# A gating stage over sorted edges: BF16 one-hot products in place of a dense count matrix

## The chip, the cores and the metric

The kernel runs on one core of one Trainium2 chip. The metric is the device time in microseconds (us) of one execution. The engines' short names are those of the profile: PE is TensorE (PEld its weight loads), DVE is VectorE, ACT is ScalarE, POOL is GpSimd, SP is SyncE, which here only issues DMAs (SPq is its queue, POOLq that of GpSimd). SBUF is the on-chip memory of 128 partitions, PSUM the accumulator that PE writes, HBM the memory outside.

## The reference

The program is two layers of a graph network over N = 3125 nodes with D = 256 features. Each layer adds to x a graph convolution and an attention mixer, and then a mixture of experts. Only the first layer's expert part, `_L0_ffn_ref`, is computed in another way by the change; cut to what matters:

```python
x = x + _L0_gnn_ref(xn, edge_index, ...) + _L0_mix_ref(xn[None], ...)[0]
x = x + _L0_ffn_ref(_layernorm(x)[None], ...)[0]

def _L0_ffn_ref(x, ..., edge_index):          # M = 3125 nodes, 65536 edges, 4 heads, 4 experts
    h = (x_flat @ W_gat).reshape(M, HEADS, NUM_EXPERTS)
    src = concatenate([edge_index[0], arange(M)]); dst = concatenate([edge_index[1], arange(M)])
    a_src = (h * att_src).sum(-1);  a_dst = (h * att_dst).sum(-1)
    e = leaky_relu(a_src[src] + a_dst[dst], negative_slope=0.2)
    ee = exp(e - segment_max(e, dst)[dst])
    alpha = ee / (segment_sum(ee, dst)[dst] + 1e-16)
    agg = segment_sum(h[src] * alpha[:, :, None], dst).reshape(M, 16) + b_gat
    scores = layernorm(agg).reshape(M, HEADS, NUM_EXPERTS).mean(1)
    topk_s, topk_i = top_k(scores, 2);  w = softmax(topk_s)
    for ei in range(NUM_EXPERTS):
        g = where(topk_i == ei, w, 0.0).sum(-1)
        hh = gelu(x @ W1[ei] + b1[ei])                       # 256 -> 512
        out = out + g[..., None] * (hh @ W2[ei] + b2[ei])    # 512 -> 256
```

So every node attends to the sources of its incoming edges and to itself; the result only decides which two of four experts a node takes and with what weights. The edge indices of this part run to 4095: a source above 3124 counts as node 3124, and an edge with a destination above 3124 is dropped. The mixer (`_L0_mix_ref`) is four transformer blocks with linear attention: Q, K, V from a layer norm, and a feed-forward part of 1024 hidden units.

## The kernel before

Nodes stand in tiles of 128: NT = 25 tiles `t`, the last with 53 rows, and NG = 7 groups `g` of four tiles (512 columns). All stages run one after the other on the core, and the engines overlap inside a stage. Instructions are issued in order on each engine; a planner places them.

**Start and mixer** (0 to 1732 us). x is loaded and normed for all groups; then four layers `l`, each a QKV part (25 tiles, `beside()` after each tile) and a feed-forward part (`experts_hidden`, then the second product with `add_row`; `beside(2)` after each tile). One call `beside(n)` is n slots, 75 slots a layer, 300 in all. Two generators are advanced there beside the mixer's own work, at a rate per slot that `OF_GRAPH` and `OF_GATING` set:

- `graph.places` and `graph.blocks` count the 100000 edges of the graph convolution into a matrix A (BF16, HBM) with one-hot products: per block of eight columns DVE makes `g_ol` and `g_oh` (L544), PE multiplies (L551), ACT copies out (L555), a DMA stores.
- `windows(eb, tail)` does the 65536 gating edges, 512 columns of 128. For each column DVE compares a key with five columns of keys, `junk<-kr,keyb,w_before` (L324), which tells how often an edge occurs; `counted` turns this into a place; POOL adds the value into the N x N count matrix C2 in HBM by an indirect DMA (L336). The DMAs go in windows of five, each after the one before has landed. `clear_own` zeroes C2 first (L619, 25 DMAs).

**Graph convolution** (1732 to 2020 us). xn is read back from HBM (`xg<-xn_d`, L214) and split into three BF16 parts `xb` (L980 to L985); a branch `if_more()` covers counts that BF16 can't hold; then `sums` multiplies them by A (L920).

**Gating and experts of layer 0** (2020 to 3112 us), in three steps:

1. Each group is normed and turned, its features go to HBM (`xf_d`), and `hg` = x W_gat, a_src and a_dst are made.
2. "gat0", 2109 to 2484 us: for each of the 25 target tiles the rows of C2 are read (`cnt`, L1167), ACT makes a penalty (`pen`, L1171), and DVE takes for four heads the maximum of a_src over the sources (L1174). Beside this `experts()` computes all four experts for all nodes (L235 with `xfg`, L1100) and stores the results in HBM (`y_d`).
3. "gat1", 2484 to 3112 us: for all pairs of target and source columns and all heads the softmax terms are made densely: ACT (L1260, L1277), POOL (L1261) and DVE (L1266, L1284) on 128 x 1024 tiles, counts turned by PE (L1282), sums by PE (L1296). `weighed` makes the gates and adds the experts' results, read back from `y_d`, with diagonal products (L1468, L1469).

**Layer 1** (3112 us to the end) is a second graph convolution, mixer and expert part.

The rate of the two side generators is all there is to it in the loop:

```python
for i, (it, w) in enumerate(((counting, OF_GRAPH), (gating, OF_GATING))):
    if not (clearing and i):
        share[i] += w * n
    while share[i] >= 1.0:
        share[i] -= 1.0
        next(it, None)
```

Of the kernel before, what the change touches and what calls it, by code (L numbers as in the profile page):

```python
# [8 lines left out]
F32 = mybir.dt.float32  # L9
# [8 lines left out]
P = 128  # L18
# [21 lines left out]
WIDE = 5  # L40
BLOCK = 6 * WIDE
COLS = 32
MANY = 9
# [12 lines left out]
GT = 3  # L56
OF_GRAPH = 1.05
OF_GATING = 0.45
# [33 lines left out]
def tile_gps(ctx: ExitStack, tc: tile.TileContext, a, out):  # L92
# [31 lines left out]
    masks = {}  # L124
    for w in (32, 64):
        m = ctile([P, P], f"mask{w}")
        V.memset(m, 0.0)
        for i in range(P // w):
            V.memset(m[i * w:(i + 1) * w, i * w:(i + 1) * w], 1.0)
        masks[w] = m  # L130
# [3 lines left out]
    xf_d = dram.tile([P, 2, N], F32, name="xf_d")  # L134
# [4 lines left out]
    pq_d = dram.tile([10, N], F32, name="pq_d")  # L139
    y_d = dram.tile([NT, P, 4, D], F32, name="y_d")  # L140
# [87 lines left out]

    def experts_hidden(ps, pool, w1, xT, n, nhb, bias, bufs=10):
# [69 lines left out]
    class Edges:  # L299

        after = mybir.DependencyInfo(mybir.DependencyClass.Sync, mybir.DependencyReason.DATA)

        def __init__(self, ep, w_before, dump, key, width, used, rows, mat, tag):
            self.ep, self.w_before, self.dump = ep, w_before, dump
            self.key, self.used, self.rows = key, used, rows
            self.flat = mat.rearrange("(n o) -> n o", o=1)
            self.val = ep.tile([P, width], F32, name=f"val{tag}", tag=f"val{tag}")
            self.idx = key[:, :].bitcast(I32)
            self.before, self.started = [], []
            self.width, self.made = width, 0  # L310

        def prepare(self, cols):

            ep, key = self.ep, self.key
            c0, c1 = self.made, min(self.made + cols, self.width)
            for c in range(c0, c1, WIDE):
                k = min(WIDE, c1 - c)
                kr = ep.tile([P, WIDE * P], F32, name="kr", tag="kr", bufs=2)
                nc.sync.dma_start(kr[:, :k * P], self.rows[c * P:(c + k) * P]
                                  .rearrange("(o f) -> o f", o=1).to_broadcast([P, k * P]))  # L320
                for j in range(k):
                    junk = ep.tile([P, WIDE * P], BF16, name="junk", tag="junk", bufs=1)
                    u = (WIDE - 1 - j) * P
                    V.scalar_tensor_tensor(junk[:, :k * P], kr[:, :k * P], key[:, c + j:c + j + 1],  # L324
                                           self.w_before[:, u:u + k * P], op0=OP.is_equal, op1=OP.mult,
                                           accum_out=self.val[:, c + j:c + j + 1])
                if c + k < c1:
                    yield
            counted(key, self.val, self.dump, c0, c1 - c0)
            self.made = c1  # L330
            yield

        def scatter(self, c, end):

            assert c < self.made
            s = G.indirect_dma_start(  # L336
                out=self.flat, out_offset=bass.IndirectOffsetOnAxis(ap=self.idx[:, c:c + 1], axis=0),
                in_=self.val[:, c:c + 1], in_offset=None, compute_op=OP.add)

            first, last = c == 0, c == self.used - 1  # L340
            if not first and not last:
                for o in self.started:
                    tc.declare_no_dep(s.ins, o.ins, reason="no index twice in a window")
# [4 lines left out]
            if end:  # L348
                self.before, self.started = self.started, []
# [1697 lines left out]
```

## Time and profile before

| what | value |
|---|---|
| time, median of 3 runs | 4495.22 us (4488.73 to 4502.27) |
| the profiled execution | 4501.24 us, of which the span from first to last instruction is 4499.5 us |
| granted PE clock, mean | 0.923 |
| busy share of the span | PE 85%, DVE 57%, ACT 35%, POOL 35% |
| first QKV product starts at | 67.3 us |
| mixer's QKV parts, layers 0 to 3 | 67 to 216, 534 to 629, 952 to 1055, 1379 to 1468 us |
| gating's compares (L324) run from, to | 249.9 to 1278.7 us |
| gating's indirect DMAs (L336) run from, to | 256.9 to 1624.8 us |

Times are counted from the first instruction of the profiled execution. A row of a stage gives, for each engine, the us in which it was busy in that stretch and in brackets how many instructions. A row of a group gives line, engine, operation, what is written and read, shapes and count; then busy us in all, mean ns of one; then the idle time just before such instructions and what ended it. A busy PE isn't a PE at its peak: one of its matmuls overlaps the next, so the distance from start to start is shorter than the length shown.

### The profile page before, as it was taken

The numbers are of one execution on the slowest core, as the hardware profiler recorded it, in microseconds if no ns is written. First come the engines' busy times: TensorE is split into PE (matmuls) and PEld (weight loads), VectorE is DVE, ScalarE is ACT, GpSimd is POOL, SyncE is SP. The second block draws the span as 40 slices with busy tenths as digits, with TensorE's granted clock in tenths as the row PEclk, the third lists the DMA queues.
The fourth block names the chain that finished last, engine by engine and source line by source line (L and its number), as shares of the span: only waits on it lengthen the run. The fifth ranks groups of instructions, "written<-read, shape, count | busy, mean of one in ns | idle before, by whom it ended". The sixth has DMA issues, their size and how long they took to land. (4 is left out here: it accounts for less than half of the span.)

```text
span 4499.5 us, 48886 instructions
## 1 busy us (share of the span) xinstructions
PE 3841.9 (85%) x17539; PEld 2271.2 (50%) x17630; DVE 2580.8 (57%) x6382; ACT 1566.8 (35%) x2431; POOL 1563.1 (35%) x1044
## 2 busy tenths in 40 slices
PE   3589979997999898988996465767899989999998
PEld 2366655665666564445664222323554444444577
DVE  7687887878766322024999899998710313223331
ACT  3232432343234322013544698984300210000133
POOL 0345555656555620000000588884000310000134
PEclk9799989998999999997998687988999999999999
DMA  9946555564545213225554322324622122211366
GB/s 275 269 58 54 61 43 52 59 56 47 53 30 46 4 3 102 70 71 195 182 195 127 127 91 87 110 89 153 200 72 75 54 77 60 59 54 56 109 166 161
DMA packets 432666, 433.19 MB, mean 96 GB/s; under 512 B 203827, under 2 KB 367958, under 8 KB 427304
## 3 DMA queue, kind: packets, MB, share of 16 engines
q1 hardware_dynamic: 345826, 413.75, 35.9%
q0 software_dynamic: 86576, 16.09, 7.4%
q8 instruction: 146, 2.39, 0.2%
q14 instruction: 118, 0.97, 0.1%
HBM read 300.31 MB, written 136.76 MB: 97 GB/s over the span
## 5 line engine op out<-in xcount | busy, mean ns | idle before, releaser
L336 POOL DMA_INDIRECT C<-valb,keyb x512 | 812.5, 1587 | 632.8 <-DMA C<-valb,keyb 298.5
L1261 POOL TENSOR_TENSOR ex<-ex,pqb 128x1024 f32<-128x1024 f32 (+1 forms) x150 | 353.6, 2378 | 943.4 <-ACT ex L1260 943.1
L324 DVE SCALAR_TENSOR_TENSOR junk<-kr,keyb,w_before 128x640 bf16<-128x640 f32 x512 | 446.8, 873 | 9.5 <-DMA kr<-keys_b 7.0
L920 PE MATMUL ag<-chb,Hb 128*128 128x512 bf16 (+1 forms) x1752 | 412.9, 386 | 17.2 <-DMA chb<-A 15.2
L920 PE MATMUL ag<-chb,xb 128*128 128x512 bf16 (+3 forms) x1907 | 397.9, 365 | 15.6 <-DMA chb<-A 12.9
L1174 DVE CUSTOM_DVE_ANT_0 am<-asb,pen 128x1664 f32<-128x1664 f32 (+3 forms) x200 | 357.2, 1786 | 51.7 <-ACT pen L1171 41.8
L872 PE MATMUL o<-w,hid 128*128 128x256 f32 (+1 forms) x1600 | 380.1, 386 | 0.0
L235 PE MATMUL mm<-hT,w 128*128 128x512 f32 (+1 forms) x896 | 375.1, 566 | 1.8 <-ACT hid L238 1.8
L1296 PE MATMUL pa<-ex,hgp 128*32 128x512 f32 (+1 forms) x1200 | 196.1, 731 | 179.1 <-DVE ex L1284 178.8
L238 ACT ACTIVATE hid<-mm,fm 128x512 f32<-128x512 f32 (+1 forms) x336 | 210.5, 631 | 395.6 <-PE mm L235 393.1
L1284 DVE SCALAR_TENSOR_TENSOR ex<-ex,ct 128x2048 f32<-128x2048 f32 (+1 forms) x150 | 336.2, 2277 | 6.8 <-PE ct L1282 5.0
L872 PEld LDWEIGHTS o<-w,hid 128*128 128x128 f32 (+1 forms) x1600 | 295.5, 191 | 52.5 <-issue 10.5
L1277 ACT ACTIVATE ex<-ex,as 128x1024 f32<-128x1024 f32 x300 | 319.8, 1134 | 2.7 <-DVE ex L1266 2.6
L920 PEld LDWEIGHTS <-xb 128*128 128x128 bf16 (+1 forms) x2100 | 183.4, 97 | 231.5 <-issue 22.3
L920 PEld LDWEIGHTS <-Hb 128*128 128x128 bf16 (+1 forms) x2100 | 184.1, 99 | 226.9 <-issue 33.7
L235 PEld LDWEIGHTS mm<-hT,w 128*128 128x128 f32 x896 | 159.5, 195 | 163.2 <-issue 149.9
L1576 POOL DMA_INDIRECT slots<-rb,r_ati x50 | 50.4, 1007 | 510.5 <-DVE rb L1569 402.9
L769 PE MATMUL mm<-wqkv,hT 128*128 128x512 f32 (+1 forms) x400 | 209.8, 642 | 7.4 <-DVE kmax L783 6.4
L551 PE MATMUL gc<-g_oh,g_ol 128*128 128x50 bf16 (+1 forms) x1589 | 177.4, 273 | 36.3 <-ACT g_st L555 35.0
L235 PE MATMUL mm<-xfg,f0w 128*128 128x512 f32 (+1 forms) x448 | 189.5, 568 | 16.2 <-DMA xfg<-xf_d 11.4
L555 ACT ACTIVATE g_st<-gc 128x400 bf16<-128x400 f32 x192 | 95.1, 503 | 292.9 <-DMA A<-g_st 144.0
L551 PEld LDWEIGHTS <-g_ol 128*128 128x128 bf16 (+1 forms) x1589 | 157.8, 146 | 68.9 <-issue 55.8
(489 smaller groups left out, 6189.2 us busy)
## 6 DMA issues: line engine op xcount, KB each, us to landing
C<-zero SPq DMA_DIRECT2D x25, 1528.0 KB
cnt<-C SPq DMA_DIRECT2D x24, 1562.5 KB
cd<-C SPq DMA_DIRECT2D x36, 1024.0 KB
kr<-keys_b SPq DMA_DIRECT2D x102, 320.0 KB
f1w<-in_f_w_dram SPq DMA_DIRECT2D x56, 512.0 KB
slots<-blank SPq DMA_DIRECT2D x15, 1820.0 KB
chb<-A SPq DMA_DIRECT2D x48, 397.2 KB
A<-g_st SPq DMA_DIRECT2D x24, 768.0 KB
```

Source lines behind the costliest of these rows:

```text
L235: T.matmul(ph[:, :n], lhsT=w1[:, k, hb * P:(hb + 1) * P], rhs=xT[:, k, :n], start=(k == 0), stop=(k == 1))
L238: S.activation(h[:, :n], ph[:, :n], AF.Gelu, bias=bias[hb])
L324: V.scalar_tensor_tensor(junk[:, :k * P], kr[:, :k * P], key[:, c + j:c + j + 1], self.w_before[:, u:u + k * P], op0=OP.is_equal, op1=OP.mult,
L336: s = G.indirect_dma_start(out=self.flat, out_offset=bass.IndirectOffsetOnAxis(ap=self.idx[:, c:c + 1], axis=0), in_=self.val[:, c:c + 1], ...
L551: T.matmul(p[:, j, :], lhsT=lo[:r, :, j], rhs=hi[:r, :h, j], start=True, stop=True)
L769: T.matmul(pqk[:r], lhsT=h, rhs=wqkv[:, k, 0:512], start=(k == 0), stop=(k == 1))
L872: T.matmul(po[:r], lhsT=hid[hb][:, j * P:j * P + r], rhs=w2[:, hb, :], start=(hb == 0), stop=False)
L920: T.matmul(acc[fb, g][:, :n], lhsT=Xb[:r, s, i, fb * P:(fb + 1) * P], rhs=ch[:r, at:at + n], start=first, stop=last, skip_group_check=g == ...
L1174: V.tensor_tensor_reduce(out=junk[:r, :w], in0=asb[:r, h, c0:c1], in1=pen[:r, :w], scale=1.0, scalar=-3.0e38, op0=OP.subtract, op1=OP.max, ...
L1261: G.tensor_tensor(e, e, pq[:r, h, :n], op=OP.add)
L1277: S.activation(ex[:r, h, :n], ex[:r, h, :n], AF.Exp, bias=sc)
L1284: V.scalar_tensor_tensor(e4, e4, 1.0, ct[:r, None, :m].to_broadcast([r, 4, m]), op0=OP.min, op1=OP.mult)
```

## The change

In words, along the program:

- **C2 and its clearing leave the common path.** `Edges`, `windows`, `clear_own` and the ordered adding DMAs go. Instead `Buckets` sorts the gating edges by pair of tiles: the key of an edge is (tile of dst) x 29 + (tile of src), times 128, and each key owns 128 places (640 where the source tile is the last) of a table `btab` in HBM. `split` makes keys and in-tile offsets (a word dst x 128 + src). `places` runs over 128 steps of WIDE = 4 columns, in three parts each: DVE compares keys (as before, now four columns wide, all that came earlier counting 1) and makes one-hot rows `od`, `os_` of the tile numbers; PE turns `od` (four products), ACT copies the result, PE multiplies `od` with `os_` (four) and the turned rows with the running counts (four); DVE adds the two ranks and updates the counts. Every 32 columns the places are computed and POOL writes the words with 32 indirect DMAs, which add nothing and have no order among them (512 in all, as before). The last 32 come after the last step.
- **The rates.** `OF_GATING` goes from 0.45 to 1.4; gating has 25 parts for every 32 columns, 400 in all. Up to slot `HEAD` = 18 only the graph's generator runs, at 2.5 a slot.
- **The start.** The load of x is issued first; only group 0 is normed before the loop, the others inside `normal`; the loading and first steps of the lists move into the generator `begun`.
- **Before the first graph convolution** the table is read back (`wf<-btab`), taken apart into two BF16 rows of in-tile offsets, stored (`low_d`), and one of them turned (`to_low`). In the order of SP's queue the load of `wf` stands after two of the seven loads of `xg` and waits for the last indirect DMA.
- **Step 1 of the gating** keeps the features in SBUF (`xT`) and computes expert 0 for each group beside it.
- **gat0 and gat1 go.** `sparse()` runs over 725 chunks of 128 places, six at a time (121 blocks): `fetched` loads two rows of offsets to all partitions and makes one-hot matrices (`hot`, twice, and `put`, 128 x 768 BF16); `gathered` picks a_src, h and a_dst with two BF16 products per chunk (the tables are split into three BF16 parts), and DVE, ACT (Exp) and POOL make the terms, with the node's own edge's e in the place of the maximum; `added` sums a chunk into its target tile with a third product. The blocks are stepped from `keep_beside` beside the last group of expert 0 and expert 1; the order of the built program has 45 of 121 blocks between these experts' products, and 76 after them.
- **Experts.** Results of experts 0 and 1 stay in SBUF (`y`); the gates are made for all tiles at once; experts 2 and 3 run last, and `weigh` adds them straight from PSUM with the gate as a scale. The bias is a small BF16 product in each tile (`ones3`, `rows0`).
- **A branch** `if_more(dense)` holds the dense attention (`in_full`) for inputs in which a bucket overflows or a_src lies beyond 30.
- ACT's activation tables: the built program of the changed kernel has 50 table loads, before 12; of the 50, 43 stand at Gelu (25) and at the new Exp (18).

The core of the diff:

```diff
-WIDE = 5
-BLOCK = 6 * WIDE
+WIDE = 4
...
-OF_GATING = 0.45
+OF_GATING = 1.4
+CHUNKS = 29
...
+SOME = 6
+HEAD = 18
...
+        def places(self, ps, w_before):
...
+            for c0 in range(0, E1 // P, COLS):
...
+                    kr = ep.tile([P, WIDE * P], F32, name="kr", tag="kr", bufs=2)
+                    nc.sync.dma_start(kr, keys_g[c * P:(c + WIDE) * P]
+                                      .rearrange("(o f) -> o f", o=1).to_broadcast([P, WIDE * P]))
+                    for j in range(WIDE):
+                        junk = ep.tile([P, 5 * P], BF16, name="junk", tag="junk", bufs=1)
+                        u = (WIDE - 1 - j) * P
+                        V.scalar_tensor_tensor(junk[:, :WIDE * P], kr, self.key[:, c + j:c + j + 1], w_before[:, u:u + WIDE * P],
+                                               op0=OP.is_equal, op1=OP.mult, accum_out=rank[:, c - c0 + j:c - c0 + j + 1])
+                    od, os_ = (ep.tile([P, WIDE, HIS], BF16, name=f"b_{nm}", tag=f"b_{nm}", bufs=2) for nm in ("od", "os"))
+                    for o, of in ((od, self.dh), (os_, self.sh)):
+                        V.tensor_tensor(o, self.of[:, None, :].to_broadcast([P, WIDE, HIS]),
+                                        of[:, c:c + WIDE, None].to_broadcast([P, WIDE, HIS]), op=OP.is_equal)
+                    yield
+                    for j in range(WIDE):
+                        T.transpose(turned[:, j * P:(j + 1) * P], od[:, j, :], ident_b)
+                    to = ep.tile([P, WIDE * P], BF16, name="b_to", tag="b_to", bufs=1)
+                    S.activation(to[:HIS], turned[:, :WIDE * P], AF.Copy)
+                    for j in range(WIDE):
+                        T.matmul(made, lhsT=od[:, j, :], rhs=os_[:, j, :], start=(j == 0), stop=(j == WIDE - 1))
+                    yield
+                    for j in range(WIDE):
+                        T.matmul(found[:, j, :], lhsT=to[:HIS, j * P:(j + 1) * P],
+                                 rhs=self.counts[:HIS].rearrange("p k h -> p (k h)"), start=True, stop=True)
+                    was = ep.tile([P, 5 * P], BF16, name="b_was", tag="junk", bufs=1).bitcast(F32)
+                    was = was[:, :2 * HIS * WIDE].rearrange("p (w k h) -> p w k h", w=WIDE, k=2)
+                    V.tensor_tensor(was, found.rearrange("p w (k h) -> p w k h", k=2),
+                                    os_[:, :, None, :].to_broadcast([P, WIDE, 2, HIS]), op=OP.mult)
+                    more4 = ep.tile([P, WIDE], F32, name="b_more", tag="b_more")
+                    V.tensor_reduce(more4, was.rearrange("p w k h -> p w (k h)"), axis=AX.X, op=OP.add)
+                    r4 = rank[:, c - c0:c - c0 + WIDE]
+                    V.tensor_tensor(r4, r4, more4, op=OP.add)
+                    n, parts2 = self.total[:HIS], self.counts[:HIS]
+                    V.tensor_tensor(n, n, made, op=OP.add)
+                    V.tensor_copy(parts2[:, 0, :], n)
+                    V.tensor_tensor(parts2[:, 1, :], n, parts2[:, 0, :], op=OP.subtract)
+                    yield
...
+                for c in range(c0, c0 + COLS):
+                    d = G.indirect_dma_start(
+                        out=btab.rearrange("(n o) -> n o", o=1),
+                        out_offset=bass.IndirectOffsetOnAxis(ap=self.key[:, c:c + 1].bitcast(I32), axis=0),
+                        in_=self.word[:, c:c + 1], in_offset=None)
...
+            nc.sync.dma_start(wf[:, :full, :], btab[0:full * P * P].rearrange("(b p s) -> p b s", p=P, s=P))
...
+                nc.sync.dma_start(low_d[i].rearrange("(b p s) -> p b s", p=P, s=P), wb[:, i])
...
+            def fetched(k0, n):
...
+                    nc.sync.dma_start(row[:, :n * P], low_d[i:i + 1, k0 * P:(k0 + n) * P].to_broadcast([P, n * P]))
...
+                    V.tensor_scalar(h[:, :n * P], row[:, :n * P], own[:, 0:1], None, op0=OP.is_equal)
...
+                V.tensor_tensor(put[:, :, :n], all6[:, :, :n], to_low[:, None, k0:k0 + n].to_broadcast([P, P, n]),
+                                op=OP.is_equal)
...
+            def gathered(k0, n, hot, put):
...
+                for j in range(n):
+                    dh, k = (k0 + j) // CHUNKS, (k0 + j) % CHUNKS
+                    T.matmul(pg[:, 60 * j:60 * j + 60], lhsT=hot[1][:, j * P:(j + 1) * P],
+                             rhs=tables[0][:, min(k, HIS - 1)], start=True, stop=True)
+                    T.matmul(pg[:, 360 + 24 * j:384 + 24 * j], lhsT=hot[0][:, j * P:(j + 1) * P],
+                             rhs=tables[1][:, dh], start=True, stop=True)
...
+                V.tensor_reduce(vs[:, :n], pg[:, :60 * n].rearrange("p (j k v) -> p j v k", k=3, v=20), axis=AX.X, op=OP.add)
+                V.tensor_reduce(vd[:, :n], pg[:, 360:360 + 24 * n].rearrange("p (j k v) -> p j v k", k=3, v=8),
                                 axis=AX.X, op=OP.add)
+                e = vs[:, :n, 0:4]
+                V.tensor_tensor(e, e, vd[:, :n, 0:4], op=OP.add)
+                V.scalar_tensor_tensor(e, e, 0.2, e, op0=OP.mult, op1=OP.max)
+                V.tensor_tensor(e, e, vd[:, :n, 4:8], op=OP.subtract)
+                S.activation(e, e, AF.Exp)
+                m = vs[:, :n, 4:20].rearrange("p j (h v) -> p j h v", h=4)
+                V.tensor_tensor(m, m, e[:, :, :, None].to_broadcast([P, n, 4, 4]), op=OP.mult)
...
+                S.activation(mp3[:, :n, 0], vs[:, :n], AF.Copy)
+                G.tensor_tensor(rest[:, :n], vs[:, :n], mp3[:, :n, 0], op=OP.subtract)
+                S.activation(mp3[:, :n, 1], rest[:, :n], AF.Copy)
+                G.tensor_tensor(mp3[:, :n, 2], rest[:, :n], mp3[:, :n, 1], op=OP.subtract)
...
+                    T.matmul(acc[dh], lhsT=put[:, :, j], rhs=mp3[:, j].rearrange("p k v -> p (k v)"),
+                             start=(k == 0), stop=(k == CHUNKS - 1))
...
+            def keep_beside(e):
+                def done(t, r, po):
+                    nonlocal share1
+                    S.activation(y[:r, e, t, :], po[:r], AF.Copy)
+                    share1 += each1
+                    while share1 >= 1.0:
+                        share1 -= 1.0
+                        next(beside1, None)
+                return done
...
+            def weigh(e):
+                def done(t, r, po):
+                    V.scalar_tensor_tensor(xs[:r, t, :], po[:r], gt[:r, t, e:e + 1], xs[:r, t, :], op0=OP.mult, op1=OP.add)
```

## The prediction

> **What bounds the kernel now.** I read the busy time by stages first, since no engine bounds the whole span: two stretches of the mixer's feed-forward part, then the two gating steps.
>
> ```profile
> core 0: us, PE busy (x) PEld busy (x) DVE busy (x) ACT busy (x) POOL busy (x), PEclk, DMA share, GB/s
> 1510.00:1730.00 220.00, 218.40 (x841) 138.57 (x840) 48.04 (x171) 56.71 (x98) 72.81 (x47) 1.00 0.16 5
> 1055.00:1379.00 324.00, 289.51 (x1343) 198.10 (x1341) 230.86 (x711) 96.82 (x168) 194.18 (x123) 0.93 0.49 45
> 2109.00:2484.00 375.00, 326.37 (x1173) 211.35 (x1171) 362.61 (x455) 175.42 (x253) 0.00 (x0) 0.95 0.50 170
> 2484.00:3112.00 628.00, 404.97 (x2338) 165.62 (x2338) 560.38 (x524) 521.54 (x518) 467.40 (x261) 0.82 0.32 100
> ```
>
> The mixer is bound by PE: its last feed-forward part, with neither graph nor gating beside it, is 99% PE; with both it takes 324 us, PE 89%. gat0 is bound by DVE (363 of 375), with the four experts' products beside it at no cost; gat1 by DVE with ACT and POOL close behind. Next I read the costliest groups, for what goes and for durations of what comes:
>
> ```profile
> L324 DVE SCALAR_TENSOR_TENSOR junk<-kr,keyb,w_before 128x640 bf16<-128x640 f32 x512 | 446.8, 873 | 9.5 <-DMA kr<-keys_b 7.0
> L1174 DVE CUSTOM_DVE_ANT_0 am<-asb,pen 128x1664 f32<-128x1664 f32 (+3 forms) x200 | 357.2, 1786 | 51.7 <-ACT pen L1171 41.8
> L1284 DVE SCALAR_TENSOR_TENSOR ex<-ex,ct 128x2048 f32<-128x2048 f32 (+1 forms) x150 | 336.2, 2277 | 6.8 <-PE ct L1282 5.0 <-ACT ex L1277 1.4
> L235 PE MATMUL mm<-xfg,f0w 128*128 128x512 f32 (+1 forms) x448 | 189.5, 568 | 16.2 <-DMA xfg<-xf_d 11.4 <-ACT hid L238 4.6
> L1100 PE MATMUL o<-f0w,hid 128*128 128x256 f32 (+1 forms) x800 | 181.7, 380 | 1.5 <-ACT hid L238 0.8 <-ACT yo L1102 0.7
> L551 PE MATMUL gc<-g_oh,g_ol 128*128 128x50 bf16 (+1 forms) x1589 | 177.4, 273 | 36.3 <-ACT g_st L555 35.0 <-ACT hT L203 0.9
> L544 DVE TENSOR_TENSOR g_ol<-g_all,g_lo 128x1024 bf16<-128x1024 bf16 (+1 forms) x199 | 136.0, 683 | 0.0
> L927 PE MATMUL ag<-ident_b,xb 128*128 128x128 bf16 x144 | 8.9, 219 | 0.0
> L434 POOL DMA_INDIRECT g_t<-tab,g_idx x25 | 24.3, 972 | 19.4 <-DVE g_skip L473 9.3 <-issue 6.4 <-DVE g_t L506 3.1
> L238 ACT ACT_TABLE_LOAD x6 | 7.7, 1283 | 0.1
> ```
>
> A small BF16 product costs 8.9/144 = 0.06 us (L927) to 177.4/1589 = 0.11 (L551, weights read with a stride). An expert costs PE (189.5 + 181.7)/4 = 93 us.
>
> **A, the start: -70.** The first QKV product comes at 67.3 us; DVE waits there for a late row (17.57 us in the timeline):
>
> ```profile
> 60.01 0.43 DVE L681 CAST row_part<-row_x 128x512 bf16<-128x512 f32 x1 [17.57 <-DMA row_x<-in_mix_rows_dram]
> ...
> 60.47 0.35 DVE L682 TENSOR_SCALAR rows<-row_part,row_pick 128x512 bf16<-128x512 bf16 x1
> ```
>
> With x first: 4.0 MB of x and QKV weights at the 268 GB/s that the first 64 us show, 15 us, plus two norms of one group (eight L176 of 0.41, 22 small ones at 0.2, eight L187 of 0.59), 12: about 27, so -40. Layer 0's QKV part takes 149 us, the others 89 to 103; clearing C2 (25 x 1528 KB, 143 us of DMA) goes out of it, the norms of six groups (22 us of DVE) come in: 115, so -34, rounded to -70 in all. Ends -30 and -85.
>
> **B, gating beside the mixer: +153.** DVE loses 447 + 42 (accumulator reads) + 16 (places), and gains 512 compares of 512 (L324's 879 ns at 640 and 481 at 256 give 745), 424 with their reads, plus 128 x 1.5 us of small ones and 22 of places: +131 on 1122 busy of 1668. That stays off the bound. PE is the bound, and had none of this: 128 iterations of 12 small products at 0.08 us are 0.96, and changes between FP32 and BF16 add some 0.4 (a bias row L690 makes a distance of 0.41 in a run of 0.216): 1.35 us, 173 in all. By layer: 26, 34, 34 and 34 iterations. Layer 1 needs 329 us of PE without side work (67 of QKV, 262 of feed-forward as in layer 3), 55 of graph and now 46: 430, at 96% busy 448, against 418 (534 to 952): +29. Likewise layer 0 gets +35 and layer 2 +25; layer 3 ran without gating (L324 ends at 1279) in 354 us and becomes 329 + 20 of graph + 46 over 0.96, 410: +56. The four parts left over after the last slot (283 x 1.4 = 396 of 400): +8. The new waits: PE's third group waits for ACT's copy, behind Gelus of 0.63, and all of the mixer's products queue behind it; DVE's rank update waits for PE. Ends: +70 (PE's idle 11% takes it) and +260 (2.2 us an iteration). POOL's 512 DMAs without adding cost 0.97 each (L434) instead of 1.59, in no order; nothing waits but the next item.
>
> **C, reading the table back: +36.** The last 32 DMAs start after the mixer, 32 x 0.97 = 31 us, landing 3.5. SP's load of `wf` waits for them; behind it in SP's queue stand five of seven `xg` loads, and for those PE, ACT and DVE with `xb`, then every load of A. The 26 us that the loads and `xb` took (1732 to 1758) hide two groups. Ends +10 and +60.
>
> **D, gating and experts: 1092 becomes 825, -267.** gat0 (375), gat1 (628) and the 89 ahead go. In their place:
> - Norms and turning (45 us alone before) beside six groups of expert 0: PE-bound, 130, and 5 for the rows.
> - The sparse pass. A block on DVE: two `hot`, one `put`, reductions of 360 and 144 from PSUM, three operations on 24 elements, one on 96. `put` by L544: 0.55. Reductions by L775 (0.419 at 256): 0.53 and 0.30; small ones 0.165 (rsqrt's), 0.25 the last. For `hot` the row L682 gives 0.35 at 512, so 0.48 at 768. [...] Sum 3.1, with gaps 3.2. PE needs 12 x 0.06 + 6 x 0.11 + 0.3 = 1.7 a block; POOL two of 0.44. The two rows of 196 KB that a block loads are 123 GB/s, under half of the 268 that the start shows, and are asked for three blocks ahead. So the 76 blocks alone are DVE-bound, 243. The 45 beside expert 1: PE 103 + 4 + 77 = 184, DVE 144.
> - [...] Gelu and Exp now alternate, 36 switches. [...] By the row, with DVE waiting for Exp at part of them: 215 in place of 184. [...]
> - Filling the pipeline costs 7, for the first rows and the first chain; gates for all tiles in one chain of some 40 DVE operations of 0.2 to 0.5, 17, plus the branch, 8 (before the first graph sums, `if_more()` and the first loads take 12 together, 1758.6 to 1770.6): 25, with PE mostly waiting, since two tiles' results fill its accumulators before the gates are there. Experts 2 and 3: 2 x 93 + 50 biases x 0.3 = 200; `weigh`'s 100 DVE operations of 0.42 lie beside.
>
> Sum 130 + 5 + 215 + 243 + 7 + 25 + 200 = 825. Ends 740 (DVE 2.7 a block) and 960 (4.3). Layer 1 is the same.
>
> What the removed steps moved (C2 read twice, 75 MB; `xf_d` and `y_d`) was hidden, so its going is worth nothing by itself.
>
> **Total.** 4501 - 70 + 153 + 36 - 267 = 4353 against the profiled execution's own 4501; the median of the runs shown is 6 less, so 4347, forecast 4345. Its own range is 4270 to 4430.
>
> **Rivals.**
> - *The mixer stalls* (0.12). The three dependent groups of each iteration sit in PE's one queue; if each makes PE wait for ACT and DVE, an iteration costs 4 us, 339 more: 4690, slower. It decides from (4501 - 4353)/128 = 1.2 us more an iteration, 2.5. For: ACT's Gelus of 0.63 lie in the way. Against: PE waited for ACT's g_st only 35 us in 199 blocks.
> - *The sparse pass runs at the latency of its chain* (0.14): products, two reductions, three small ones, Exp, two copies with POOL's differences. At 4.3 us a block, 121 x 1.1 more: 4485, even. For: Exp waits behind table loads. Against: `hot` of a block is issued a whole block ahead.
> - *Cheaper* (0.20): PE's idle share takes gating (+70) and DVE needs 2.7 a block (-60): 4210.
> - *The dense branch is taken* (0.01): 65536 edges make about 64 a bucket, places 128, a deviation of 8; it would add thousands of us.
>
> The forecast has 0.53. Within 0.3% (what a measurement here tells from no change) is 4482 to 4509: 0.05, mostly the second rival; slower 0.13, faster 0.82. The range 4190 to 4500 leaves out the first rival and some of the rest.
>
> **What would show it.** First QKV product near 27 us; mixer's end near 1815; `wf` landing some 40 us later; 3.2 us from block to block with DVE over 90% busy after expert 1; ACT loads of 1.28. Wrong if layer 3 exceeds 450 us, or the sparse pass 600.

## The result, and the profile after

On the chip on which both kernels were first timed together, the changed kernel took **4745.11 us** (median of 4 runs, 4739.49 to 4746.85), the kernel before 4492.93 (4 runs): a ratio of 1.0556, 95% interval 1.0536 to 1.0576. It is slower there, where 4345 was forecast, and the range, 4190 to 4500, does not hold it.

This number can't be read without one more: of the five chips that the experiments ran on, this same kernel took 4270 to 4279 us on four (on one of them under the name e1_spread, whose queues hold the same instructions), against 4447 to 4453 of the kernel before (0.960, interval 0.957 to 0.964), and 4719 against 4453 on the fifth. Both outcomes have to be explained.

The same stages as before, in the first profile after. Columns: the window in us, its length, busy time of each engine with its instructions, granted TensorE clock, DMA share, GB/s. In this order: feed-forward of layer 3, feed-forward of layer 2, and the three stretches that stand where gat0 and gat1 stood (expert 0 with the norms, the sparse pass, experts 2 and 3):

```profile
core 0: us, PE busy (x) PEld busy (x) DVE busy (x) ACT busy (x) POOL busy (x), PEclk, DMA share, GB/s
2024.00:2312.00 288.00, 232.27 (x999) 141.62 (x998) 113.07 (x444) 59.64 (x103) 61.40 (x64) 0.89 0.08 18
1379.00:1779.00 400.00, 321.21 (x1569) 210.10 (x1569) 214.36 (x779) 104.53 (x184) 95.15 (x96) 0.87 0.24 29
2641.00:2769.00 128.00, 116.78 (x472) 74.73 (x473) 35.78 (x195) 43.45 (x85) 2.47 (x2) 0.92 0.11 33
2769.00:3153.00 384.00, 210.48 (x2531) 154.71 (x2530) 301.78 (x1083) 168.04 (x480) 112.38 (x243) 0.68 0.52 120
3153.00:3369.00 216.00, 200.79 (x683) 119.10 (x682) 87.61 (x257) 40.21 (x62) 0.00 (x0) 0.95 0.03 11
```

The lower three rows show that the new gating and experts work: 128 + 384 + 216 = 728 us in place of 1092. The upper two show where the time went: the mixer. It ends at 2312 in place of 1732, PE is busy for 80% of a feed-forward part and no other engine for more than 54%. Nothing is saturated: every engine waits.

The granted clock in 40 equal slices of the span, from the page, says the same: the mixer is the first 19 to 20 digits, and they change between 7 and 9 where the last ten are all 9.

```profile
PEclk7779877898878888798799897569999999999999
```

**Where they wait.** POOL issues the 512 scatters of the table in 16 stretches of 32. This is the timeline of ACT around the third of them, which lasts from 621.2 to 661.3 (start, duration, instruction; in brackets the idle time ahead of it and what ended that):

```profile
624.00 0.31 ACT L260 ACTIVATE hid<-mm,fm 128x53 f32<-128x53 f32 x1 [0.55 <-PE mm L257]
626.47 0.59 ACT L403 ACTIVATE b_to<-bp 25x512 bf16<-25x512 bf16 x1 [2.15 <-PE bp L401]
631.92 0.78 ACT L209 ACTIVATE hT<-tr,fm 128x512 f32<-128x512 f32 x1 [4.87 <-PE tr L207]
635.46 0.78 ACT L209 ACTIVATE hT<-tr,fm 128x512 f32<-128x512 f32 x1 [2.77 <-remote]
644.65 0.50 ACT L639 ACTIVATE g_st<-gc 128x400 bf16<-128x400 f32 x1 [8.42 <-remote]
665.69 0.50 ACT L639 ACTIVATE g_st<-gc 128x400 bf16<-128x400 f32 x1 [20.53 <-remote]
...
667.28 0.48 ACT L639 ACTIVATE g_st<-gc 128x400 bf16<-128x400 f32 x1
```

"remote" is the page's word for a wait that no record on this core ends. The ACTIVATE at 665.69 waits for one thing, the semaphore that PE counts up behind its eight products L635. Products and copies go in turn, one to one: the products of 648.07 are copied at 667.28, and those of this copy are the eight before, which the timeline of PE shows over at 637.2:

```profile
636.29 0.92 PE L635 MATMUL gc<-g_oh,g_ol 128*128 128x50 bf16 x8 [1.73 <-issue]
...
646.52 0.60 PE L401 MATMUL bp<-ident_b,b_od 128*25 128x128 bf16 x4 [6.62 <-DVE g_oh L628]
...
648.07 0.95 PE L635 MATMUL gc<-g_oh,g_ol 128*128 128x50 bf16 x8
667.16 0.26 PE L405 MATMUL bp<-b_os,b_od 128*25 128x25 bf16 x4 [18.14 <-ACT b_to L403]
```

The count rises at 665.66, 28 us behind these products and 16.6 behind the last product that PE had begun; ACT reads it, copies `b_to`, and only then PE goes on with L405. From 649 on PE, VectorE and ACT all stand still. The profile models the ends of products, but PE began others from 637.03 to 648.75, so it wasn't held by these. The measure for the whole trace is the distance of a rise from the last product ahead of it, which is the least that it can be late: up to the first product of the graph step 62 rises come over 1 us behind, up to 25 us. On the four chips that take 4270 to 4279 none does, of 1385.

### The profile page after: what moved, and what is told of

Its sections match the earlier page's. It is cut to its first block, busy times and chain, and to the rows that moved or that the text cites. A ratio compares the mean times of both kernels' runs of the same rounds, so it can differ in the third digit from the quotient of the medians.

```text
span 4744.8 us, 52978 instructions
## 1 busy us (share of the span) xinstructions
PE 3793.8 (80%) x18969; PEld 2287.3 (48%) x19060; DVE 2138.0 (45%) x7790; ACT 1165.8 (25%) x2366; POOL 897.6 (19%) x1029
## 5 line engine op out<-in xcount | busy, mean ns | idle before, releaser
L434 POOL DMA_INDIRECT btab<-b_word,b_key x512 | 500.3, 977 | 1692.3 <-DVE b_key L432 848.1
L937 PE MATMUL o<-w,hid 128*128 128x256 f32 (+1 forms) x1600 | 418.6, 404 | 30.2 <-issue 16.5
L393 DVE SCALAR_TENSOR_TENSOR junk<-kr,b_key,w_before 128x512 bf16<-128x512 f32 x512 | 376.2, 735 | 6.1 <-DMA kr<-keys_g 4.8
L833 PE MATMUL mm<-wqkv,hT 128*128 128x512 f32 (+1 forms) x400 | 231.3, 690 | 43.8 <-issue 18.6
L1188 PE MATMUL o<-f0w,hid 128*128 128x256 f32 (+1 forms) x800 | 207.8, 397 | 4.8 <-ACT hid L260 4.5
L257 PE MATMUL mm<-xT,f0w 128*128 128x512 f32 (+1 forms) x448 | 194.1, 571 | 13.2 <-DMA f0w<-in_f_w_dram 10.1
L628 DVE TENSOR_TENSOR g_ol<-g_all,g_lo 128x1024 bf16<-128x1024 bf16 (+1 forms) x199 | 136.2, 684 | 144.6 <-remote 92.3
L940 DVE TENSOR_TENSOR xs<-xs,o 128x256 f32<-128x256 f32 (+1 forms) x100 | 41.9, 419 | 351.3 <-PE o L750 306.1
L207 PE MATMUL tr<-ident,rows 128*128 128x128 f32 (+1 forms) x500 | 93.6, 320 | 132.7 <-ACT rows L193 94.8
L635 PE MATMUL gc<-g_oh,g_ol 128*128 128x50 bf16 (+1 forms) x1589 | 178.7, 273 | 22.5 <-ACT g_st L639 9.6
L635 PEld LDWEIGHTS <-g_ol 128*128 128x128 bf16 (+1 forms) x1589 | 158.0, 147 | 63.6 <-issue 43.8
L1304 PE MATMUL acc<-mp,put 128*128 128x60 bf16 x725 | 56.2, 222 | 143.2 <-POOL mp L1294 142.2
L1188 PEld LDWEIGHTS o<-f0w,hid 128*128 128x128 f32 (+1 forms) x800 | 143.5, 190 | 42.8 <-issue 11.4
```

Of the source, the lines that this page charges most:

```text
L207: T.transpose(p[:, j * P:j * P + r], x[:, c * P:(c + 1) * P], ident[:r, :r])
L257: T.matmul(ph[:, :n], lhsT=w1[:, k, hb * P:(hb + 1) * P], rhs=xT[:, k, :n], start=(k == 0), stop=(k == 1))
L393: V.scalar_tensor_tensor(junk[:, :WIDE * P], kr, self.key[:, c + j:c + j + 1], w_before[:, u:u + WIDE * P], op0=OP.is_equal, op1=OP.mult, ...
L434: d = G.indirect_dma_start(out=btab.rearrange("(n o) -> n o", o=1), out_offset=bass.IndirectOffsetOnAxis(ap=self.key[:, c:c + 1].bitcast(I ...
L628: V.tensor_tensor(o[:r, :w, :k], self.all[:r, :w, :k], of[:r, None, c:c + k].to_broadcast([r, w, k]), op=OP.is_equal)
L635: T.matmul(p[:, j, :], lhsT=lo[:r, :, j], rhs=hi[:r, :h, j], start=True, stop=True)
```

## The experiments

Runs of one set are on one chip. The chip of the result is called A, those of the five sets B to F (A may be one of them). The names of the theories are those of the expectations.

**First set (chip B): is it the bursts of scatters, or the iteration's chain?**

*e1_spread* was to issue the scatters between the steps of the iterations.

```diff
-                for c in range(c0, c0 + COLS):
-                    d = G.indirect_dma_start(
...
+                ready.extend(range(c0, c0 + COLS))
                 yield
...
                         T.matmul(made, lhsT=od[:, j, :], rhs=os_[:, j, :], start=(j == 0), stop=(j == WIDE - 1))
+                    scattered(1)
                     yield
```

> The changed kernel with the 32 scatters of a group of columns no longer issued one behind another but one, one and two at the three steps of each of the next eight iterations; the last group's 32 stay together. Theory 'burst' (while POOL issues 32 scatters back to back, 1.26 us apart, the signals between the other engines stall; PE stands idle about 300 us in 16 such places): the stalls go, mixer's end near 2030 instead of 2312, total 4460 to 4520. Theory 'each scatter' (every scatter takes a fixed time from the others wherever it stands): 4745, no change within 30. Theory 'chain' (the recorded rival: PE waits in each iteration for ACT and DVE): 4745, no change within 20.

Measured: 4272.8 us (4 runs), 0.9601 of before (0.9581 to 0.962). The mixer ends at 1838.2. That was less than any theory gave, and the reason was not the edit: POOL's scatters wait for nothing that the steps make, so its queue ran ahead of the text and the bursts stood as before, 32 in a row. In the traces every engine has the same instructions as in the changed kernel. The run told something else: this program, unaltered, has two outcomes.

*e2_noscat* leaves the scatters out, and so the table (the sparse pass runs on an empty one).

```diff
-                    d = G.indirect_dma_start(
-                        out=btab.rearrange("(n o) -> n o", o=1),
...
                 yield
```

> The changed kernel without the 512 scatters (it leaves out writing the table of edges, so the sparse pass runs on an empty table; only its time up to the table is read). Theory 'burst' and theory 'each scatter': mixer's end near 2030, total about 4430 (the wait for the table behind the mixer, about 40 us, goes too). Theory 'chain': mixer's end stays near 2300, total about 4705.

Measured: 4245.95, the mixer's end at 1822.2. On this chip 512 scatters cost the mixer 16 us beside the same work, 0.03 each.

*e3_norank* leaves out the ranking across columns and gives each edge a place outside the table.

```diff
-                    for j in range(WIDE):
-                        T.transpose(turned[:, j * P:(j + 1) * P], od[:, j, :], ident_b)
...
-                    V.tensor_tensor(parts2[:, 1, :], n, parts2[:, 0, :], op=OP.subtract)
+                    yield
+                    yield
...
-                V.scalar_tensor_tensor(sel, rank, -float(CAPS[0]), sel, op0=OP.add, op1=OP.is_lt)
+                V.scalar_tensor_tensor(sel, rank, BAD, sel, op0=OP.add, op1=OP.is_lt)
```

> The changed kernel without the ranking across columns: one-hot rows, transposes, ACT's copy, both groups of products and the updates on VectorE are left out; the compares within four columns and all scatters stay (every edge goes to a place of its own outside the table, so the sparse pass runs on an empty table). Theory 'burst': only the products' own time goes, 128 x about 1.3 us: mixer's end near 2140, total about 4575. Theory 'chain': nearly all of the 627 us by which the mixer grew over its old length goes: mixer's end near 1700, total about 4150.

Measured: 4369.17, the mixer's end at 1950.5, later than with the ranking. It answers neither theory: without the chain the compares were scheduled ahead (the last at 1354 in place of 1844), and ACT then waited 160 us between 500 and 1340 for stores of the graph's `g_st`, which SP issues. It is no measure of the ranking's cost.

*e4_late* sets the rate of gating beside the mixer to nothing.

```diff
-OF_GATING = 1.4
+OF_GATING = 0.0
```

> The changed kernel with no gating beside the mixer: all 128 iterations and all scatters run behind the mixer. Mixer without gating: ends near 1600 to 1680. Theory 'burst': an iteration alone costs VectorE's 4.8 us, 614 in all, plus up to 20 us in each of 16 bursts: 614 to 930 behind the mixer, total 4650 to 5050. Theory 'chain': each iteration is a serial chain of 8 us or more: 1020 or more, total 5050 or more.

Measured: 4640.17. The mixer ends at 1678.8, with 21 of the 128 iterations in it; behind it stand 614 us. The difference to e1, whose mixer ends at 1838.2 with 126 iterations in it, measures what one costs there: 105 more make it 159 us longer, 1.52 each, of which 1.31 is busy time of PE (1484 us in e4's mixer, 1621 in that of e5 below). POOL issued 448 scatters in one row behind the mixer, 1.26 us apart, and no engine stopped. The chain theory is out on this chip.

**Second set (chip C): the same program again.**

*e5_again_a* and *e6_again_b* are the changed kernel with no edit, *e7_spread_b* and *e8_norank_b* the kernels of e1 and e3.

> The changed kernel as it is, once more. The queues of e1_spread turned out to hold the same instructions in the same order with the same waits as those of the changed kernel (POOL's scatters wait for nothing between the steps, so moving them in the text moved nothing), and yet it took 4273 in place of 4745. Theory 'state' (one program, two outcomes: in some runs PE's signals come up to 27 us late while POOL issues scatters, in others not): about 4270 or about 4745, nothing between. Theory 'text' (something that differs between the two files decides): 4700 to 4750 here. Theory 'chip' (it goes by the chip): all three like programs of this call agree.

> The same kernel as e5_again_a under another label. Theory 'state': about 4270 or about 4745, and it need not agree with e5_again_a. Theory 'text': 4700 to 4750. Theory 'chip': as e5_again_a.

> The kernel of e1_spread once more, the same instructions as e5_again_a. Theory 'state': about 4270 or about 4745. Theory 'text': 4260 to 4285. Theory 'chip': as e5_again_a.

> The kernel of e3_norank once more (the ranking across columns left out, the table empty), which showed 17 us stalls in eight bursts of scatters and 4369. Theory 'state': either 4369 again, or without stalls about 120 less, 4250. Theories 'text' and 'chip': 4369 on the same chip.

Measured: 4275.95, 4278.6 and 4272.64, ratios 0.9603 (0.9568 to 0.9639), 0.9609 and 0.9596; e8 4356.54. "Text" falls: the file that took 4745 takes 4276. All three like programs agree, and in every other set the programs with these scatters either all stall or none does, so it goes by the chip, or by the moment. e8 repeats e3, whose waits for `g_st` are another thing: none of PE's signals is late in either.

The third stretch of scatters in e5, by windows, and the time without scatters behind it. Below them, the like pair of the first profile after.

```profile
540.00:582.00 42.00, 39.65 (x210) 24.16 (x209) 27.18 (x101) 19.39 (x39) 31.34 (x31) 0.90 0.55 96
582.00:622.00 40.00, 35.00 (x180) 20.68 (x179) 34.22 (x141) 17.95 (x39) 0.00 (x0) 1.00 0.33 42
```

```profile
621.00:662.00 41.00, 17.51 (x78) 10.17 (x78) 6.38 (x22) 3.56 (x7) 30.66 (x32) 0.58 0.21 59
667.00:713.00 46.00, 42.42 (x204) 25.04 (x203) 34.58 (x133) 20.90 (x44) 0.00 (x0) 0.93 0.37 47
```

With POOL at the same work (31 and 32 scatters, 31 us busy), PE gets 210 instructions done in one and 78 in the other, VectorE 101 and 22, while the windows without scatters are alike. Over all fifteen stretches of scatters inside the mixer, each counted up to 6 us behind its end, PE is busy 680 of 719 us in e5 (95%) and 325 of 705 in the slow profile (46%); outside them it is busy 93% in both. That accounts for the 474 us by which the slow profile is longer from 232 to the mixer's end: 341 are PE's idle time in those stretches, 38 its idle time elsewhere, and 95 are longer busy time (the mean clock is 0.85 there in place of 0.95).

**Third set (chip D): traces of both kernels on one chip, and two remedies.**

*e9_again_c* is the changed kernel, *e10_before* the kernel before, *e11_rate* the one edit below, and *e12_paced* that edit and a copy on POOL that was to hold back each four scatters.

```diff
-OF_GATING = 1.4
+OF_GATING = 1.6
```

```diff
+                    if ready:
+                        G.tensor_copy(pace, more4[:, 0:1])
+                        scattered(4)
                     yield
```

> The changed kernel as it is, on whatever chip this set gets. Theory 'chip' (the late signals of the first measurement belong to the chip or moment it ran on): about 4275 with mixer's end near 1838 where the kernel before takes about 4450, or about 4745 with mixer's end near 2312 where the kernel before takes about 4493. Theory 'state' (any run may show them): 4745 possible beside 4450 as well.

> The kernel before as it is, for a trace beside that of the changed kernel on the same chip. Theory 'chip': the 45 us by which it is shorter on these chips (4450 in place of 4493) lie in the mixer, where POOL issues its 512 adding scatters: mixer's end near 1690 in place of 1732. If they lie behind the mixer, the scatters are not what slows it on the first chip.

> One change: OF_GATING 1.6 in place of 1.4, so that gating ends some 35 of 283 slots ahead of the mixer's end and its last 32 scatters run beside the mixer. If step C (reading the table back) is the wait for the last scatters, the first graph product comes about 40 us behind the mixer's end in place of 80: total 4235. If the wait is SP's queue or the load itself, no change: 4275.

> As e11_rate, and in each iteration POOL first copies one number that VectorE has just made and then issues four scatters, so that bursts of 32 become groups of four (a dependence does what the place in the text could not). On a chip without late signals: 4235, the same as e11_rate within 15, since bursts cost nothing there. On a chip with them, theory 'burst': near 4300, while e11_rate takes about 4700.

Measured: 4718.86, 4458.47, 4727.88 (1.0603, 1.0574 to 1.0631) and 4707.02 (1.0571, 1.0545 to 1.0596). This chip stalls: 61 late signals of PE in e9 by the measure above, and the mixer ends at 2287.2, much as on A. In e11 the first graph product follows the mixer's end by 35 us in place of 80, as expected of step C, but the total is that of e9. e12 decides nothing, since its scatters still follow each other every 1.27 us, in rows of up to 32; its 21 us less than e11 are not explained. The trace of the kernel before is worth most. On this same chip its mixer ends at 1692.5 and it takes what it takes on the others, with as many scatters:

```profile
L336 POOL DMA_INDIRECT C<-valb,keyb x512 | 814.7, 1591 | 592.9 <-DMA C<-valb,keyb 279.5 <-issue 188.4 <-DMA kr<-keys_b 71.6
```

Those add, take 1591 ns, follow each other every 1.86 us and go in windows of five. None of PE's signals is late beside them, so scatters as such don't stop a chip that stalls. But the same trace has four late ones, up to 8 us, at another place: at the 25 gathers of the graph's list (`g_t<-tab`, indirect DMAs of POOL as well, which don't add and follow each other every 1.25 us). Here is ACT's copy of four products of PE beside them, on D (the first two rows) and in the profile before:

```profile
171.59 0.39 PE L513 MATMUL gt<-ident_b,g_hib 128*128 128x128 bf16 x4
180.93 0.60 ACT L516 ACTIVATE g_lo<-gt 128x512 bf16<-128x512 bf16 x1 [5.71 <-remote]
...
170.89 0.39 PE L513 MATMUL gt<-ident_b,g_hib 128*128 128x128 bf16 x4
171.32 0.60 ACT L516 ACTIVATE g_lo<-gt 128x512 bf16<-128x512 bf16 x1 [1.28 <-PE gt L513]
```

The copy comes 9 us behind the products in one and 0.04 in the other. The changed kernel has the same 25 gathers, with four late signals each on A (up to 18.5 us) and D (up to 21.4), and none on the other chips. So the kernel before stalls on D too, where it issues plain indirect DMAs; the change puts 512 more of them beside the mixer. The profile before has no late signal up to the graph step. On which chip it was taken isn't on record: its 4501 us lie in the range of A, but it is none of the four executions timed there. Its mixer ends at 1732.5, 40 us later than on D, and that difference is not explained.

**Fourth and fifth set (chips E and F): rate or kind of the scatters.**

*e14_slow* puts five small operations of POOL ahead of each scatter, *e15_add* and *e17_add_b* let the scatters add, *e13_again_d* and *e16_again_e* are the changed kernel, *e18_rate_b* that of e11.

```diff
                 for c in range(c0, c0 + COLS):
+                    still = [G.memset(pace, 0.0) for _ in range(5)]
+                    if spread:
+                        tc.add_manual_dep(still[0].ins, spread[-1].ins.name, behind, reason="pace")
                     d = G.indirect_dma_start(
...
+                    tc.add_manual_dep(d.ins, still[-1].ins.name, behind, reason="pace")
                     spread.append(d)
```

```diff
             V.scalar_tensor_tensor(word, di, float(P), si, op0=OP.mult, op1=OP.add)
+            V.tensor_scalar(word, word, -float(P * P), None, op0=OP.add)
...
-                        in_=self.word[:, c:c + 1], in_offset=None)
+                        in_=self.word[:, c:c + 1], in_offset=None, compute_op=OP.add)
```

> The changed kernel as it is: the measure for the other two of this set. On a chip like the first: about 4720 to 4745 with 40 or more of PE's signals over 1 us late; on the other kind: about 4276 and none.

> POOL clears a tile of 128x128 five times ahead of each scatter, held in this order by dependences, so that scatters follow each other every 2.3 to 2.8 us in place of 1.26; the same 512 scatters otherwise. Where e13_again_d stalls: theory 'rate' (the stall needs the quick succession of POOL's DMAs) 4300 to 4400; theory 'each scatter' (each costs the others a fixed time) about 4720; theory 'kind' (plain scatters do it, adding ones don't) about 4720. Where e13_again_d does not stall: 4276 to 4310 by each.

> The scatters add, as those of the kernel before did (the value has the table's start value taken off first, one operation on VectorE), which makes one take 1.55 us and follow each 1.85. Where e13_again_d stalls: theory 'kind' 4290 to 4340, theory 'rate' between 4300 and 4500, theory 'each scatter' about 4720. Where it does not: 4276 to 4310 by each.

> The changed kernel as it is, to tell the kind of chip: about 4720 to 4745 with late signals of PE, or about 4275 with none.

> The kernel of e15_add once more. Where e16_again_e stalls: theory 'each scatter' about 4720; theories 'rate' and 'kind' under 4500. Where it does not: 4295 again.

> The kernel of e11_rate once more. Where e16_again_e does not stall: step C's wait for the last 32 scatters (a 40 us stretch behind the mixer in which all engines stand still in e13_again_d, 98 in e14_slow, 63 in e15_add, in step with the length of the last burst) is covered by the mixer: 4235. If SP's load of the table is the wait, 4275. Where it stalls: about 4725.

Measured: e13 4270.58 and e16 4269.79, so neither chip stalls, and rate and kind are not told apart. e14 took 4326.2 (0.9727, 0.9699 to 0.9756), over the 4310 expected because its last row of scatters is the longest, e15 4295.24 (0.9658, 0.9627 to 0.9688), e17 4291.9 (0.9645, 0.9615 to 0.9675), e18 **4261.01** (0.9577, 0.9554 to 0.9599), the fastest complete kernel measured, on a chip that doesn't stall.

The traces do settle step C. Behind the mixer all engines stand still until SP's load of `wf` lands, and that stretch follows the length of the last 32 scatters: 40 us in e13 and e16 (1.26 us apart), 63 in e15 and e17 (1.85), 98 in e14 (2.39). SP's queue in e14, where the engines stand still from 1846 to 1944:

```profile
1940.69 0.37 SPq L1051 DMA_DIRECT2D wf<-btab  x1
1941.10 0.42 SPq L1052 DMA_DIRECT2D wf<-btab  x1
1941.64 5.28 SPq L220 DMA_DIRECT2D xg<-xn_d  x2
```

Its last scatter starts at 1938.5, and the loads of `xg` queue behind `wf`, as the prediction said. In e18 the stretch is gone, but the mixer ends at 1868 (1833 in e16 on the same chip), since all its iterations now lie inside: of 40 us, 12 are left at the first graph product (1902.5 against 1914.1 in e16) and 9 at the end.

## Why the prediction was wrong, and where it was right

**The step that failed** stands at the end of part B: "POOL's 512 DMAs without adding cost 0.97 each (L434) instead of 1.59, in no order; nothing waits but the next item." Their price held (977 ns), and no instruction of the mixer waits for them. But on chips A and D the engines stand still while POOL issues them, about 25 us in each stretch of 32 by PE's idle time, and the mixer's end came 474 us later than on B (2312 against 1838). Layer 3, for which the prediction named 450 us as a sign of being wrong, took 531. The prediction priced a DMA issue on an idle engine by its own duration, and had no rival in which issuing disturbs engines that wait for nothing of it.

**The rival that came nearest in time was not the cause.** "The mixer stalls", 4690, named PE's waits for ACT and VectorE in the iteration's chain. Those waits are in the first profile (18.14 us of PE for ACT's `b_to` in the row above), but as the consequence of late signals. Where no signals are late an iteration costs 1.52 us, far from the 4 of the rival and near the 1.35 of the sum.

**On the four chips that do not stall, the sum held.** It gave 4353 against 4501, a ratio of 0.967; the runs give 0.960. That the two lie so close is in part luck. Against the profile from which the sum started, e5 is 223 us shorter and not 148, since D was over-priced by 97 while the start and the mixer were under-priced by 24 and C by 7, and layer 1 is 8 shorter; and the kernel before takes some 45 us less on these chips too, which brings the ratio back. By its steps, on e5 unless another is named:
- A: the first QKV product comes at 20.1 (predicted 27). But layer 0's QKV part ends at 217.7, where it ended at 216.7 before: the 47 us gained at the start were lost again, as PE waits 62 us there for rows that ACT normalizes (L193). ACT in turn waits for VectorE, which between 40 and 90 us has 24 compares of the graph's list (L511, 20.8 us) among its norms; the sum had no term for this work, which the change moved into the loop. The predicted -70 left nothing at that point, and layer 0 ended at 551 where the sum has 495 (27 + 467 - 34 + 35).
- B: 1.31 us of PE an iteration against 1.35, and layer 1 takes 448 us against 448. Layer 2 takes 441 and layer 3 400, both about 10 less than its 452 and 410. So they gave back about 20 of layer 0's 56, and the mixer ends at 1839.5 against 1815 (the 8 for the last parts lie behind it).
- C: from the mixer's end to the first graph product 81 us in place of 38, +43 against +36, by the mechanism named.
- D: 728 us against 825. Expert 0 with the norms 128 against 135, experts 2 and 3 216 against 225. The sparse pass was over-priced, 384 against 465: one block takes 3.22 us beside expert 1 (43 blocks), where the sum had PE decide at 4.8 (215 over 45), and 3.04 alone, where it had 3.2. Of the 215, 31 us over PE's 184 are the author's estimate of VectorE's waits at the 36 switches, from the 1283 ns of a table load (L238); no run shows them. In the first profile after, the 50 loads take 1283 ns each, 41 stand within 0.02 us of both neighbours, and VectorE waits for Exp (L1286) 3.2 us in all. Nor does a run show the 2.7 a block of the part's lower end and of the rival "Cheaper", an estimate too.

The term for `hot`, 0.48 us, came near by luck. `hot` takes 453 ns in the mean and 416 in the median, but the step by which the prediction went from 512 results (0.35, L682) to 768, 0.13 us, is twice what the traces show. In the first profile after, the like operation of L245 takes 283 ns for 256 results and 349 for 512, and `hot` 416 for 768: 66 and 67 ns for 256 more, or 0.26 ns a result. By an estimate from these three, about 0.2 us of each is a fixed part.

The rows of the first profile after, in which busy us and the mean of one in ns stand behind the bar:

```profile
L434 POOL DMA_INDIRECT btab<-b_word,b_key x512 | 500.3, 977 | 1692.3 <-DVE b_key L432 848.1 <-issue 273.7 <-DVE b_os L397 174.6
...
L393 DVE SCALAR_TENSOR_TENSOR junk<-kr,b_key,w_before 128x512 bf16<-128x512 f32 x512 | 376.2, 735 | 6.1 <-DMA kr<-keys_g 4.8
...
L1261 DVE TENSOR_SCALAR hot<-row,own 128x768 bf16<-128x768 bf16 (+1 forms) x242 | 108.5, 453 | 5.8 <-PE pg L1275 5.8
...
L1264 DVE TENSOR_TENSOR put<-all,to_low 128x768 bf16<-128x768 bf16 (+1 forms) x121 | 68.0, 564 | 49.0 <-PE acc L1304 38.1 <-PE pg L1275 9.7
```

A scatter costs POOL 977 ns (0.97 predicted), a compare VectorE 735 (745), a `hot` 453 (0.48 us), a `put` 564 (0.55).

**What stays open.** That the stalls lie in the stretches of scatters is shown: of PE's idle stretches over 3 us in the slow mixer, 32 with 370 us lie in stretches of POOL's indirect DMAs (29 at the scatters, 3 at the gathers) and 4 with 20 us outside, beside one of 37 us at the start that e5 has too. That leaving the scatters out removes the stalls on such a chip was not run there, as no set with that kernel fell on one. Nor is it known why A and D stall and B, C, E and F don't, whether it is the chip or the moment, or whether the stall needs the quick succession of these DMAs, their kind, or many of them under way at once; on D 25 plain gathers every 1.25 us do harm and 512 adding scatters every 1.86 us, five at a time, do none. e15_add has scatters of that kind and pace, though not in windows of five, at 20 us more than e5; it is the next kernel to run on a chip that stalls.

One rival was not tested at all: that the recording of the profile takes part in the stall. The traces of A and D are themselves incomplete. Counted against the instructions that make them, the first profile after lacks 307 rises of VectorE's semaphore and 109 of ACT's (of some 6800 and 2200), nearly all in stretches of POOL's indirect DMAs, where the traces of the other four chips lack hardly any; the kernel before lacks 187 and 82 on D, there beside the adding scatters too, and none in the profile before. Every time on record comes with the clock and span of a profile, so whether an execution that isn't recorded stalls as well is open.

## What to carry to other kernels

Before an edit is blamed or praised for a change of some hundred microseconds, run the unaltered program on another chip: here the same bytes were 5.6% slower than the kernel before on one and 4.0% faster on another. In this profile, idle time that every engine shared and that ended in a "remote" wait was neither a chain nor a bound; what told was what ran in just those stretches, here POOL's DMAs, and whether the kernel before showed the same beside its own. And in e1 a change of order in the text moved nothing on an engine whose instructions wait for nothing (the scatters stood 32 in a row, as before): make the dependence, and read the order that results, before the run.

## What was unexpected of the hardware

- On A and D PE's semaphore rises up to 25 us (27 in e11) behind its last product while POOL issues plain indirect DMAs, scatters or gathers; VectorE's come up to 3.2 us late in the first profile after, ACT's never over 0.01. On the other four chips none is over 1 us late up to the graph step.
- A lower clock stands beside the idle time. The granted clock is 0.59 to 0.82 over the sixteen stretches of the first profile after (0.59 to 1.00 in e5), and PE's first products behind the third run at half the pace: four L833 in 3.78 us, then two in 1.02. Below them stand windows of the clock, PE's busy time first.

```profile
667.62 3.78 PE L833 MATMUL mm<-wqkv,hT 128*128 128x512 f32 x4
...
673.91 1.02 PE L833 MATMUL mm<-wqkv,hT 128*128 128x512 f32 x2
...
613.00:615.00 2.00, 2.00 (x19) 1.86 (x18) 1.20 (x6) 0.61 (x2) 0.00 (x0) 1.00 0.74 77
615.20:628.70 13.50, 12.25 (x47) 7.10 (x45) 4.22 (x16) 3.10 (x9) 5.74 (x6) 0.50 0.35 97
667.10:673.10 6.00, 5.94 (x17) 3.31 (x17) 6.00 (x22) 1.04 (x4) 0.00 (x0) 0.50 0.13 44
673.20:700.00 26.80, 24.88 (x136) 15.50 (x135) 17.56 (x66) 15.47 (x31) 0.00 (x0) 1.00 0.58 60
```

The record of the granted clock holds two values in this trace, 1.00 and 0.50; products L833 follow each other every 0.43 us at the one and every 0.85 at the other. What makes the clock fall and rise was not shown. It fell at 615.1 us, when PE had been busy without a gap for 10 us; 12.25 us of work in the next 13.5 did not bring it back; and behind the stall it took 6.0 us. Of the 71 falls in this trace, 21 have an idle stretch of PE of over 3 us in the 10 us ahead of them. How much of the 95 us of longer busy time the clock makes was not separated.
